# One broadcast of the packed slots per window, split into eight

## The chip, the cores and the metric

The kernel runs on one core of a Trainium2 chip. The metric is the device time of one execution in microseconds (us). Three executions of the kernel before took 478.18, 482.74 and 483.65 us; their median, 482.74 us, is what the change is compared with.

## The reference, cut to what matters

A graph layer over 6250 nodes with 128 features and 100000 edges that are sorted by destination (`dst`). Each edge has one of two types.

```python
Xs = X[src]
m_data = Xs @ W_data.T + b_data
m_ctrl = Xs @ W_control.T + b_control
msg = jnp.where((edge_types == 0)[:, None], m_data, m_ctrl)
agg = jax.ops.segment_sum(msg, dst, num_segments=X.shape[0])
out = agg + (X @ W_self.T + b_self)
x = _layernorm(X + jax.nn.relu(out), axis=-1)
```

## The kernel before, in words

**Messages first.** For all nodes and both types the products with the two weight matrices are computed once, in blocks of 128 nodes. The 98 blocks (49 for each type) stay in the tile `m3` as three bf16 parts of 128 columns each, which together carry the precision of float32, and are also written to a table in DRAM (L509). This is the first 60 us.

**Sums in two ways.** 27 windows of 160 destination nodes each are summed by matrices of zeros and ones (`ranks` and `sums`). The rest of the nodes are summed from rows that GpSimd gathers from the table by indirect transfers (`gathered`, L1027, 263 of them); their matmuls (L1034) lie between those of the windows.

**A window.** Windows are handled in eight groups: of one, of two, and six of four. For a group, `ranks` gives every edge a slot in a small list for each of the 98 source blocks, and leaves in the tile `vs` who stands in which slot. `put` (L772) writes `vs` to the DRAM tensor `packed`. For each window, `sums` then

- broadcasts that window's 32 x 98 slots to all 128 partitions of the tile `sp` (named "rows"): L904, a source of 6272 bytes written to each partition, 784 KB in all;
- lets VectorE compare `sp` with the partition's number, in two halves (L912), which gives 98 selection matrices of 128 x 32;
- lets TensorE multiply them with `m3` (stage 1, L933, 98 matmuls of 384 columns in 25 steps), ScalarE or VectorE copy each result to bf16 (L436, L437), and TensorE add these to the window's sums with a second selection, `hot2` (L920; stage 2, L947 and L950).

The tile `sp` has three buffers; a buffer is free when the stage-1 matmuls of the window three before are done. At the end `close` adds x, normalizes and stores.

**The order is planned.** All operations are entered with `add(engine, duration, function, due, reads, writes, lat)`. `Plan.run` walks through a modelled time: on each engine it takes, of the operations that are ready, the one with the smallest due time. Due times are priorities, not earliest starts. `lat` is the modelled delay until the result can be read. What comes out is a fixed order of instructions on each engine; the chip then waits on semaphores where the model was too quick. An operation on the SP queue (transfers) counts 0.45 us (`SPD`) in the model; a broadcast has `lat=2.0`. The due time of a window is `T0 + 13*w` with T0 = 36; its broadcast has due - 14 (`RA`), its compares due - 4 and due - 3.

Of the kernel before, what the change touches and what calls it, by code (L numbers as in the profile page):

```python
# [226 lines left out]
@with_exitstack  # L227
def kernel(ctx, tc, x, xt, edges, w, bias, out):
    nc = tc.nc
    const = ctx.enter_context(tc.tile_pool(name="const", bufs=1))  # L230
    total = const.tile([1, 1], I32, name="total")

    with ExitStack() as main:
        sums_over_windows(main, tc, x, xt, edges, w, bias, out, total)

    matched = nc.values_load(total[0:1, 0:1])
    with tc.If(matched != E), ExitStack() as rest:
        sums_over_all(rest, tc, x, xt, edges, w, bias, out)
# [9 lines left out]
def sums_over_windows(ctx, tc, x, xt, edges, w, bias, out, total):  # L248
# [23 lines left out]
    G0, G1 = 0.0, -4  # L272
    GC = 1.3
    SPD = 0.45
    RP, RA, RS = 1, 14, 0.9


    r0 = C([125, RH, 1], I32, "r0")
# [948 lines left out]
```

## Time and profile before

| What | us |
|---|---|
| median of three executions | 482.74 |
| the profiled execution, device time | 478.18 |
| its span, first to last instruction | 476.5 |
| TensorE busy with matmuls | 442.0 |
| VectorE busy | 393.0 |
| ScalarE busy | 354.1 |
| GpSimd busy | 298.4 |

The profiled execution is the fastest of the three; 1.7 us of its time lie outside its span. TensorE's granted clock is 0.99 of full speed in the mean. In the list of groups a line such as "L912 DVE TENSOR_SCALAR" names the line of the kernel, the engine and the operation; DVE is VectorE, ACT ScalarE, PE TensorE, POOL GpSimd. "SPq" is the queue that issues transfers in program order; a transfer that waits there holds back those behind it. In a timeline the columns are start, duration, engine, line, operation, tiles, form and count; a bracket at the end gives how long the engine stood idle before the instruction, and what ended it.

### The profile page before, as it was taken

How to read it: one execution, taken by the hardware profiler on the slowest of the kernel's cores; microseconds unless marked ns; L12 is line 12 of the kernel's file. 1: busy time of each engine (PE TensorE's matmuls, PEld its weight loads, DVE VectorE, ACT ScalarE, POOL GpSimd, SP SyncE). 2: the span in 40 equal slices, each digit the busy share in tenths (PEclk: the TensorE clock that was granted, in tenths of full speed). 3: DMA queues.
4: the chain of work that ended last, by engine and by line, in shares of the span. 5: the costliest groups of instructions: out<-in, count | busy, mean ns of one | idle time of the engine just before them, and what ended most of it. 6: DMA issues, size and time to landing. Idle time of an engine off the chain costs nothing.

```text
span 476.5 us, 26926 instructions
## 1 busy us (share of the span) xinstructions
PE 442.0 (93%) x11461; PEld 362.7 (76%) x11461; DVE 393.0 (82%) x1271; ACT 354.1 (74%) x891; POOL 298.4 (63%) x290
## 2 busy tenths in 40 slices
PE   4999988997999999999899999999999999999990
PEld 3666665775888878888788879888888887978970
DVE  6699979998999989989798998988969779554333
ACT  2476774766877976878777789777797778989981
POOL 1100017777777777777777776777777757777700
PEclk9999999999999999999999999999999999999996
DMA  5489977338463556644655446763466534746210
GB/s 147 122 233 356 300 238 211 106 91 272 142 194 83 173 180 181 186 114 112 196 183 172 113 119 186 201 179 101 124 178 191 165 84 118 229 145 182 80 44 20
DMA packets 63117, 76.83 MB, mean 161 GB/s; under 512 B 21000, under 2 KB 52893, under 8 KB 62989
## 3 DMA queue, kind: packets, MB, share of 16 engines
q1 hardware_dynamic: 49147, 47.35, 32.3%
q0 software_dynamic: 13456, 27.42, 21.7%
q8 instruction: 91, 1.49, 1.3%
q10 hardware_dynamic: 386, 0.26, 0.2%
q14 instruction: 37, 0.30, 0.2%
HBM read 60.50 MB, written 13.17 MB: 155 GB/s over the span
## 4 chain that ended last, share of the span: by engine, by line
PE 73%; DVE 10%; ACT 7%; DMA 6%; issue 2%; SPq 0%; ACTq 0%; DVEq 0%
PE g L933 20%; PE a L947 19%; PE rk L702 9%; PE ga L1034 7%; ACT gs L436 4%; PE a L950 3%; PE vt L752 3%; DMA t_msg<-table,t_idx 3%; PE g L493 3%; DMA rows<-packed 2%; DVE hot L920 2%; PE a L493 2%; ACT to_d L443 2%; DVE slot L716 2%; PE ga L702 1%
## 5 line engine op out<-in xcount | busy, mean ns | idle before, releaser
L1027 POOL DMA_INDIRECT t_msg<-table,t_idx x263 | 279.7, 1063 | 130.3 <-DVE hots L691 45.3
L436 ACT CAST gs<-g 128x384 bf16<-128x384 f32 x639 | 273.8, 481 | 73.2 <-PE g L933 55.7
L947 PE MATMUL a<-gs,hot 128*32 128x384 bf16 x2592 | 249.0, 328 | 7.7 <-ACT gs L436 5.1
L933 PE MATMUL g<-m,rows 128*32 128x384 bf16 x2646 | 253.0, 327 | 1.8 <-DVE rows L912 1.3
L933 PEld LDWEIGHTS <-rows 128*32 128x32 bf16 x2646 | 168.7, 134 | 13.1 <-DVE rows L912 1.6
L950 PE MATMUL a<-gs,hot 128*32 128x128 bf16 x1944 | 159.6, 219 | 0.2 <-issue 0.2
L947 PEld LDWEIGHTS <-hot 128*32 128x32 bf16 x2700 | 115.9, 95 | 33.9 <-issue 15.5
L1034 PE MATMUL ga<-t_msg,t_hot 128*32 128x384 bf16 x1036 | 102.0, 326 | 1.3 <-DMA t_msg<-table,t_idx 1.3
L716 DVE TENSOR_REDUCE slot<-rk 128x4 f32<-128x392 f32 (+1 forms) x138 | 76.3, 553 | 12.5 <-PE rk L702 9.8
L950 PEld LDWEIGHTS <-hot 128*32 128x32 bf16 x2025 | 82.5, 97 | 3.5 <-issue 0.4
L920 DVE TENSOR_TENSOR hot<-iota_b,to_d 128x1280 bf16<-128x1280 bf16 (+1 forms) x81 | 67.4, 842 | 0.0
L702 PE MATMUL rk<-hots,tri 128*32 128x392 bf16 (+1 forms) x588 | 59.9, 317 | 0.0
L702 PE MATMUL rk<-hots,rest 128*32 128x392 bf16 (+1 forms) x556 | 54.4, 320 | 4.9 <-DVE slot L716 3.2
L1034 PEld LDWEIGHTS <-t_hot 128*32 128x32 bf16 x1036 | 49.9, 97 | 5.5 <-issue 2.2
L912 DVE TENSOR_SCALAR rows<-rows,pid 128x1568 bf16<-128x1568 bf16 x54 | 34.2, 638 | 8.9 <-DMA rows<-packed 8.8
L691 DVE TENSOR_TENSOR hots<-iota_b,st 128x784 bf16<-128x784 bf16 (+1 forms) x83 | 38.9, 485 | 0.5 <-PE vt L752 0.4
L702 PEld LDWEIGHTS <-rest 128*32 128x32 bf16 x624 | 25.0, 96 | 14.2 <-issue 11.9
L561 DVE TENSOR_REDUCE s<-a 128x128 f32<-128x384 f32 x27 | 15.0, 556 | 24.5 <-ACT bs L436 11.0
L1021 DVE TENSOR_TENSOR t_hot<-iota_b,t_code 128x768 bf16<-128x768 bf16 (+2 forms) x47 | 24.6, 523 | 11.8 <-PE ga L1034 11.6
L702 PEld LDWEIGHTS <-tri 128*32 128x32 bf16 x672 | 28.5, 98 | 2.3 <-issue 0.2
L752 PEld LDWEIGHTS <-two 128*64 128x64 bf16 x567 | 14.4, 109 | 7.9 <-DVE two L743 3.2
L752 PE MATMUL vt<-hots,two 128*64 128x98 bf16 x546 | 17.1, 208 | 0.8 <-DVE two L743 0.4
(188 smaller groups left out, 527.1 us busy)
## 6 DMA issues: line engine op xcount, KB each, us to landing
rows<-packed SPq DMA_DIRECT2D x27, 784.0 KB
table<-m SPq DMA_DIRECT2D x12, 768.0 KB
t_msg<-table,t_idx POOLq DMA_INDIRECT x263
rows<-in_xt SPq DMA_DIRECT2D x8, 256.0 KB
xc<-in_xt SPq DMA_DIRECT2D x6, 320.0 KB
gl<-sr SPq DMA_DIRECT2D x27, 48.0 KB
xr<-in_x SPq DMA_DIRECT2D x5, 256.0 KB
out<-xr SPq DMA_DIRECT2D x5, 256.0 KB
```

The source lines that it names most:

```text
L436: [("ACT", act(cols), lambda: A.copy(o(), src())), ("DVE", dve(cols), lambda: V.tensor_copy(o(), src()))], None, None, due, r, w, lat)
L691: lambda k=k, kn=kn, ci=ci, hs4=hs4: V.tensor_tensor(hv(ci)[:, k - ks[ci] : k - ks[ci] + kn].rearrange("p k w (c d) -> p (k w) c d", d=2), ...
L702: T.matmul(acc.t[R * j : R * j + R, c * wide : c * wide + wide], wt.t[:, R * j : R * j + R], one(k).rearrange("p w c -> p (w c)"), start=s ...
L716: vec(due, len(m) * wide, lambda r=r, m=m: V.tensor_reduce(slot.t[:, r:KT:L, :], acc.t[:, : len(m) * wide].rearrange("p (k w c) -> p k w c ...
L752: T.matmul(vv()[q : q + 64, i // 2, :], two.t[:, (k - k0) * nw + i].rearrange("p f r -> p (f r)"), one(k)[:, i, :], start=k == 0 and i < 2 ...
L912: add("DVE", dve(half * NT, 0.335), lambda sp=sp, rs=rs: V.tensor_scalar(sp.t[:, rs], sp.t[:, rs], pid1.t, None, op0=ALU.is_equal), due - ...
L920: lambda i=i, hot2=hot2, s4=s4, c0=c0, c1=c1: V.tensor_tensor(hot2.t[:, c0:c1].rearrange("p g (c d) -> p g c d", d=2), iota1_b.t.rearrange ...
L933: T.matmul(gp.t[R * t : R * t + R, :D3], sp.t[:, :, 4 * g + t], m3.t[:, 4 * g + t, :], start=True, stop=True)
L947: T.matmul(a.t[R * j : R * j + R, :D3], hot2.t[:, g, R * j : R * j + R], gs.t, start=g == 0, stop=False, skip_group_check=True)
L950: T.matmul(a.t[R * c : R * c + R, D3:], hot2.t[:, g, P:], gs.t[:, c * D : (c + 1) * D], start=False, stop=last, skip_group_check=True)
L1027: add("POOL", GC, lambda m=m, kk=kk: G.indirect_dma_start(out=m.t, out_offset=None, in_=table[:, :], in_offset=bass.IndirectOffsetOnAxis(a ...
L1034: T.matmul(ga.t[R * i : R * i + R, :D3], hot.t[:, k % KB, R * i : R * i + R], m.t, start=k == 0, stop=False, skip_group_check=True)
```

## The change

One number differs: the broadcast of a window's slots is issued as eight transfers of 16 partitions each (98 KB) where it was one of 128 partitions. In the code `RP` goes from 1 to 8.

```diff
@@ -272,7 +272,7 @@
     G0, G1 = 0.0, -4
     GC = 1.3
     SPD = 0.45
-    RP, RA, RS = 1, 14, 0.9
+    RP, RA, RS = 8, 14, 0.9
```

`RP` is used in `sums` alone, at L903 to L908:

```python
for j in range(RP):
    add("SP", SPD, lambda i=i, sp=sp, j=j: S.dma_start(
        sp.t[P // RP * j : P // RP * (j + 1)].rearrange("p r c -> p (r c)"),
        packed[gi, i // 2, (i % 2) * 64 : (i % 2) * 64 + R, :]
        .rearrange("r c -> (r c)")[None, :].to_broadcast([P // RP, R * NT])),
        due - RA + RS * j, [(packed_b, gi)], [(sp, ("p", j))], lat=2.0)
```

Each piece is an operation of its own for the planner: 0.45 us of the SP queue, a due time of due - 14 + 0.9*j, and 2.0 us until it may be read. The compares of L912 read all of `sp`, so they come after the last piece. Since the order of every engine comes out of the planner, the order of other instructions can change too.

## The prediction

> **What bounds the kernel now.** I read the page's busy times first, then the engines by stretch, then the waits, then the SP queue's timeline around the broadcasts.
>
> ```profile
> span 476.5 us, 26926 instructions
> PE 442.0 (93%) x11461; PEld 362.7 (76%) x11461; DVE 393.0 (82%) x1271; ACT 354.1 (74%) x891; POOL 298.4 (63%) x290
> ```
> ```profile
> 0.00:60.00 60.00, 53.42 (x750) 34.35 (x752) 50.25 (x207) 33.42 (x70) 4.05 (x13) 1.00 0.76 232
> 60.00:125.00 65.00, 56.84 (x1487) 43.87 (x1483) 59.51 (x194) 43.55 (x116) 43.96 (x41) 1.00 0.63 184
> 125.00:440.00 315.00, 306.81 (x8581) 263.23 (x8576) 270.12 (x818) 253.74 (x648) 240.78 (x227) 1.00 0.55 156
> 440.00:477.00 37.00, 24.94 (x666) 21.23 (x655) 13.08 (x55) 23.34 (x61) 9.60 (x10) 0.87 0.18 49
> ```
> In the second view the columns after the length are busy PE, weight load, DVE, ACT, POOL, then clock, DMA share and GB/s. TensorE is the bound: from 125 to 440 us it idles 8.2 us in 315. Idle time worth having lies before 125 us (6.6 + 8.2) and in the tail (12.1), which the change does not touch. So a better broadcast can win little, and a worse one can cost as much as it pushes into TensorE.
>
> ```profile
> DVE rows L912 <- DMA rows<-packed: 8.8, 6, 2.7
> ```
> ```profile
> SPq L904 <- PE g L933: 48.9, 14, 12.1
> SPq L904 <- DMA packed<-vs: 14.1, 6, 3.3
> SPq L544 <- DMA rows<-packed: 2.2, 1, 2.2
> ```
> Most broadcasts wait in the queue for their buffer (48.9 us); the first of each group waits for `packed` (14.1 us), and there VectorE waits for the broadcast: 8.8 us in six places. How far that reaches TensorE differs:
>
> ```profile
> 70.96 0.63 DVE L912 TENSOR_SCALAR rows<-rows,pid 128x1568 bf16<-128x1568 bf16 x1 [2.16 <-DMA rows<-packed]
> ...
> 116.00 0.63 DVE L912 TENSOR_SCALAR rows<-rows,pid 128x1568 bf16<-128x1568 bf16 x1 [0.85 <-DMA rows<-packed]
> ```
> ```profile
> 72.11 0.35 PE L702 MATMUL rk<-hots,rest 128*32 128x392 bf16 x4 [1.61 <-DVE slot L716]
> ...
> 117.71 0.55 PE L933 MATMUL g<-m,rows 128*32 128x384 bf16 x8 [1.34 <-DVE rows L912]
> ```
> Twice VectorE's wait became TensorE's: 1.61 us through the rank chain that follows it, 1.34 us directly. At 228 us VectorE waited 0.67 us and TensorE not at all (6.00 of 6.00 us busy from 223 to 229). I counted off each window's 98 stage-1 matmuls and took the time from the end of its second compare to the first of them. Windows 1, 3, 7, 11, 15, 19 and 23, the first of their groups, have 2.2, 0.1, 7.5, 7.6, 6.5, 4.8 and 4.1 us; all others have 10 to 22 us.
>
> **The change, part by part.** *Instructions.* 27 broadcasts become 216, 189 more on a queue that now issues 238. Two broadcasts back to back start 0.43 us apart (109.56 and 109.99), so 189 x 0.43 = 81 us more issue time, at least. The queue has room; what counts is the train at the start of a group. Its eighth piece starts 7p after the first, p being the spacing.
>
> *The price of a piece.* No row of this trace shows a transfer to 16 partitions with 6 KB each. Nearest are trains of four short transfers to few partitions:
>
> ```profile
> 138.63 1.90 SPq L541 DMA_DIRECT2D xr<-in_x  x4
> ...
> 195.39 5.72 SPq L541 DMA_DIRECT2D xr<-in_x  x4
> ...
> 292.00 3.53 SPq L868 DMA_DIRECT2D gl<-sr  x4
> ```
> That is 0.47, 1.43 and 0.88 us for each. The queue uses eight semaphores in turn (their numbers stand in the trace's records), and a transfer waits until the last one on its semaphore has landed, which is why L544 above waited for a broadcast that it has nothing to do with; so slow pieces also slow their own issue. Bounds: p = 0.43 (issue alone) to 1.43. I take 0.88: of the three trains its transfers are the largest (48 KB against 16 KB), though part of it is a wait for the gather. From issue to landing of a short transfer 2.9 us (`packed` issued at 62.57, the broadcast that waited for it at 65.49). The last piece then lands 7p + 2.9 us after the first issue: 5.9, 9.1 or 12.9 us. Now it is 5.4 (65.49 to 70.96), 6.4 (109.56 to 116.00) and 4.9 (223.35 to 228.21).
>
> [...]
>
> *First windows of a group*, p = 0.88. Window 1: 9.1 - 5.4 = 3.7 us later, less 2.2 of slack: 1.5. Window 3: 9.1 - 6.4 - 0.1 = 2.6. Windows 7, 11, 15: up to 4.2 later, covered. Windows 19 and 23, some 3 later, covered by 4.8 and 4.1. Sum 4.1 us. At p = 0.43 it is 0 (window 1 is 0.5 later, window 3 earlier by 0.5); at 1.43 it is 5.3 + 6.4 for these two and, from the landing records of the others, 0.4 + 1.3 + 1.7 + 2.8 for windows 11, 15, 19 and 23: 18.
>
> *VectorE's order.* The planner now holds the train for 8 x 0.45 + 2 = 5.6 us instead of 2.45 and sets the compares later by 3.15 us. For a first window the chip is then late by 9.1 - 5.6 = 3.5 us, before by 5.5 - 2.45 = 3.0: about even. For a group's second window, issued just behind, the plan says 16 x 0.45 + 2 = 9.2 us after the first issue, the chip 15 x 0.88 + 2.9 = 16.1: 6.9 late; before 2.9 planned, and landed at 8.7 (the trace's landing records, 8.1 to 9.3 in five of the six groups of four): 5.8 late. That is 1.1 us more of VectorE standing still, in six groups 7 us, with evictions and rank reductions queued behind the compare. By the rows above perhaps half of such a wait reaches TensorE: 3 us. At p = 0.43 the plan's wait is longer than the real one and the term vanishes; at 1.43 it is (24.4 - 9.2 - 5.8) x 6 / 2 = 28.
>
> *The same pieces elsewhere.* Where a broadcast waits for its buffer, the train costs 3 to 6 us more of the queue, hidden by 10 to 22 us of slack. Behind it stand loads of x (due 20 us ahead), edges for later groups, and `gl`, needed in a window's last step: nothing, unless p is over 1. Window 0's broadcast lies among the table's writes but has 13 us until stage 1. GpSimd's gathers share the DMA engines; it waits for DMA 4.9 us in all and otherwise for TensorE to free its 14 buffers, so slower gathers cost nothing at first.
>
> *Sum.* 4 + 3 = 7 us on the profiled execution: 478.2 becomes 485. The median stands 4.6 us above that execution, so I put 482.7 + 7 = 490.
>
> **Rivals.** *Faster: pieces at issue speed.* With p = 0.43 the landing is as now, but VectorE's compares are planned 3.15 us later, past most of the 8.8 us of waits, and what rank work comes forward fills them. TensorE gets back at most its idle time around the broadcasts: 0.8 + 1.8 (60 to 72 us), 2.0 (110 to 123.6) and 1.2 (161 to 169), 5.8 us: 477. For it: back-to-back issues really are 0.43 us apart, and pieces leave gaps in which gathers get through. Against: the 16 engines share out 16 partitions instead of 128. It decides below p of about 0.5, where 7p + 2.9 is under 6.4.
>
> *Even.* The pieces cost about 0.6 each: 7 x 0.6 + 2.9 = 7.1, 0.7 us late at window 3, nothing elsewhere, 1 to 2 us won back on VectorE. 480 to 486. Also what a broadcast hidden by the planner's new order would look like.
>
> *Much slower.* p over 1.1: the first windows cost 3 + 4 + 1, the second (15 x 1.1 + 2.9 - 15.0) x 6 / 2 = 13, 500 and more.
>
> That the change does not do what it says is excluded but for one point: pieces could be strung out by other transfers with due times between theirs; the first windows would be later still.
>
> **How the numbers follow.** Within 1% is about what a measurement of this kernel can tell from no change. Slower by p near 0.9: 0.46, range 486 to 497. Much slower: 0.07. Even: 0.27. Faster: 0.20. The range for 8 in 10 runs from the faster case's 477 to 500, the sum at p = 1.1. Faster by over 1% (below 477.9): 0.20. Within 1%: 0.28. Slower by over 1%: 0.52.
>
> **What would show it.** Right: at group starts a train of eight L904 over 6 us or more; compares of windows 1 and 3 some 3 us later after the first issue; more VectorE time behind "DMA rows<-packed" than 8.8 us; TensorE idle before 125 us up by 4 us. Wrong: trains of 3.5 us with that wait near zero, or TensorE's idle time moving where no broadcast stands, which would be the planner's new order and not the pieces.

## The result and the profile after

| | before | after |
|---|---|---|
| median, us | 481.02 | 533.76 (533.43 to 534.08) |
| ratio | | 1.1098, 95% interval 1.1023 to 1.1172 |
| profiled span, us | 476.5 | 531.8 |

Eight pieces made the kernel 11% slower; 490 us was forecast, with a range up to 500. (A fourth execution of the kernel before took 479.31 us, so its median is 481.02 here.) Lines of the page of the kernel before, then of the changed kernel:

```profile
PE 73%; DVE 10%; ACT 7%; DMA 6%; issue 2%; SPq 0%; ACTq 0%; DVEq 0%
...
L702 PE MATMUL rk<-hots,rest 128*32 128x392 bf16 (+1 forms) x556 | 54.4, 320 | 4.9 <-DVE slot L716 3.2
...
L912 DVE TENSOR_SCALAR rows<-rows,pid 128x1568 bf16<-128x1568 bf16 x54 | 34.2, 638 | 8.9 <-DMA rows<-packed 8.8
```

```profile
span 531.8 us, 27272 instructions
...
PE 460.0 (86%) x11461; PEld 367.1 (69%) x11461; DVE 394.9 (74%) x1274; ACT 354.2 (67%) x888; POOL 301.8 (57%) x290
...
PE 53%; DMA 22%; SPq 8%; DVE 7%; issue 4%; ACT 4%; ACTq 0%; DVEq 0%; POOL 0%
...
L912 DVE TENSOR_SCALAR rows<-rows,pid 128x1568 bf16<-128x1568 bf16 x54 | 34.8, 655 | 61.4 <-DMA rows<-packed 40.9
L702 PE MATMUL rk<-hots,rest 128*32 128x392 bf16 (+1 forms) x556 | 55.5, 330 | 28.6 <-DVE slot L716 27.8
```

The work of VectorE, ScalarE and GpSimd is unchanged to about 1%. What grew is idle time: VectorE stood 61.4 us ahead of the compares, before 8.9. (The page names other releasers for a third of it; but `sp` is the only tile written by a transfer that an L912 reads, and by the landing records each of these compares started within 1 us of the landing of its own last piece.) TensorE's idle time before rank matmuls went from 4.9 to 28.6 us. On the chain that ended last, whose shares the lines with "PE 73%" and "PE 53%" give, transfers went from 6% to 22% of the span. The span grew by 55.3 us: TensorE was idle for 37.3 us more and, with the same matmuls, busy for 18.0 us more. By stretch, columns as before:

```profile
60.00:125.00 65.00, 52.78 (x1352) 39.94 (x1348) 56.54 (x185) 38.58 (x103) 41.61 (x39) 0.97 0.71 150
125.00:440.00 315.00, 280.37 (x7418) 232.70 (x7414) 244.05 (x729) 216.53 (x550) 208.88 (x194) 0.97 0.65 137
```

TensorE idles 34.6 us from 125 to 440, where it idled 8.2; the prediction looked for 4 of its 7 us before 125. One window in the middle of a group, window 13, shows how it comes about. The SP queue and VectorE in the kernel before, then the SP queue, VectorE and TensorE in the changed kernel, each from its timeline:

```profile
237.19 0.34 SPq L904 DMA_DIRECT2D rows<-packed  x1
```
```profile
244.24 0.62 DVE L912 TENSOR_SCALAR rows<-rows,pid 128x1568 bf16<-128x1568 bf16 x1
```
```profile
257.15 1.30 SPq L904 DMA_DIRECT2D rows<-packed  x1
258.55 1.10 SPq L868 DMA_DIRECT2D gl<-sr  x2
259.70 4.13 SPq L904 DMA_DIRECT2D rows<-packed  x7
```
```profile
268.56 0.69 DVE L912 TENSOR_SCALAR rows<-rows,pid 128x1568 bf16<-128x1568 bf16 x1 [2.35 <-DMA rows<-packed]
...
270.42 0.55 DVE L716 TENSOR_REDUCE slot<-rk 128x4 f32<-128x392 f32 x1
```
```profile
271.03 0.45 PE L702 MATMUL rk<-hots,rest 128*32 128x392 bf16 x4 [2.25 <-DVE slot L716]
```

Before, the broadcast landed at 243.5, 0.7 us ahead of the compare, and VectorE did not stand. In the changed kernel the first piece was issued at 257.15, the last at 262.6, and it landed at 268.5. VectorE stood 2.35 us, and the rank reduction behind the compare released TensorE 2.25 us late. Window 13's own matmuls began at 293.4, over 20 us after its compares: the window had all the slack that the prediction counted. VectorE's order had 0.7 us.

### The profile page after: what moved, and what is told of

The parts are those of the page before. It is cut to its first block, busy times and chain, and to the rows that moved or that the text cites. A ratio compares the mean times of both kernels' runs of the same rounds, so it can differ in the third digit from the quotient of the medians.

```text
span 531.8 us, 27272 instructions
## 1 busy us (share of the span) xinstructions
PE 460.0 (86%) x11461; PEld 367.1 (69%) x11461; DVE 394.9 (74%) x1274; ACT 354.2 (67%) x888; POOL 301.8 (57%) x290
## 4 chain that ended last, share of the span: by engine, by line
PE 53%; DMA 22%; SPq 8%; DVE 7%; issue 4%; ACT 4%; ACTq 0%; DVEq 0%; POOL 0%
PE g L933 16%; DMA rows<-packed 15%; PE a L947 14%; PE rk L702 6%; SPq L904 6%; PE ga L1034 5%; PE a L950 3%; PE vt L752 2%; DVE rows L912 2%; ACT gs L436 2%; DMA sr<-table,at 1%; DMA packed<-vs 1%; PE g L493 1%; DMA xc<-in_xt 1%; DMA xr<-in_x 1%
## 5 line engine op out<-in xcount | busy, mean ns | idle before, releaser
L947 PE MATMUL a<-gs,hot 128*32 128x384 bf16 x2592 | 255.6, 335 | 10.8 <-ACT gs L436 4.8
L933 PE MATMUL g<-m,rows 128*32 128x384 bf16 x2646 | 258.4, 336 | 3.9 <-issue 2.9
L933 PEld LDWEIGHTS <-rows 128*32 128x32 bf16 x2646 | 163.6, 135 | 20.4 <-issue 6.1
L950 PE MATMUL a<-gs,hot 128*32 128x128 bf16 x1944 | 162.1, 222 | 4.3 <-issue 4.3
L947 PEld LDWEIGHTS <-hot 128*32 128x32 bf16 x2700 | 118.1, 97 | 42.4 <-issue 24.9
L950 PEld LDWEIGHTS <-hot 128*32 128x32 bf16 x2025 | 82.7, 98 | 11.1 <-issue 5.9
L716 DVE TENSOR_REDUCE slot<-rk 128x4 f32<-128x392 f32 (+1 forms) x138 | 76.2, 553 | 17.5 <-PE rk L702 13.0
L912 DVE TENSOR_SCALAR rows<-rows,pid 128x1568 bf16<-128x1568 bf16 x54 | 34.8, 655 | 61.4 <-DMA rows<-packed 40.9
L702 PE MATMUL rk<-hots,rest 128*32 128x392 bf16 (+1 forms) x556 | 55.5, 330 | 28.6 <-DVE slot L716 27.8
L702 PE MATMUL rk<-hots,tri 128*32 128x392 bf16 (+1 forms) x588 | 61.3, 326 | 0.0
L1034 PEld LDWEIGHTS <-t_hot 128*32 128x32 bf16 x1036 | 48.1, 98 | 6.2 <-issue 1.9
L861 POOL DMA_INDIRECT sr<-table,at x14 | 16.4, 1169 | 10.5 <-DVE at L849 4.5
```

What stands on the lines that cost most here:

```text
L702: T.matmul(acc.t[R * j : R * j + R, c * wide : c * wide + wide], wt.t[:, R * j : R * j + R], one(k).rearrange("p w c -> p (w c)"), start=s ...
L716: vec(due, len(m) * wide, lambda r=r, m=m: V.tensor_reduce(slot.t[:, r:KT:L, :], acc.t[:, : len(m) * wide].rearrange("p (k w c) -> p k w c ...
L912: add("DVE", dve(half * NT, 0.335), lambda sp=sp, rs=rs: V.tensor_scalar(sp.t[:, rs], sp.t[:, rs], pid1.t, None, op0=ALU.is_equal), due - ...
L933: T.matmul(gp.t[R * t : R * t + R, :D3], sp.t[:, :, 4 * g + t], m3.t[:, 4 * g + t, :], start=True, stop=True)
L947: T.matmul(a.t[R * j : R * j + R, :D3], hot2.t[:, g, R * j : R * j + R], gs.t, start=g == 0, stop=False, skip_group_check=True)
L950: T.matmul(a.t[R * c : R * c + R, D3:], hot2.t[:, g, P:], gs.t[:, c * D : (c + 1) * D], start=False, stop=last, skip_group_check=True)
```

## The experiments

The indented paragraphs are the expectations, recorded before the run they belong to. They name five theories: A, a piece to 16 neighbouring partitions is slow; B, the number of transfers on the SP queue costs; C, the planner's new order costs; D, VectorE stands at compares that the plan put too early; E, the pieces cost in some other way too.

"Lands" is the time from the first piece's issue to the last piece's landing, from the trace's semaphore records; medians over the first windows of the six groups of four, the second windows (counted from the first window's first issue) and the rest. "Wait" is VectorE's idle time ahead of L912 on the page. The waits are read from the profiled executions (of h1 485.8, of h3 529.8, of k2 506.0 us), the times are medians.

| run | lands: first, second, rest | wait | median | ratio, interval |
|---|---|---|---|---|
| before | 5.7, 8.9, 5.8 | 8.9 | 481.02 | |
| h1, order alone | 5.6, 8.3, 5.5 | 0.8 | 481.23 | 0.997, 0.9926 to 1.0015 |
| k2, four pieces | 7.2, 11.2, 8.6 | 30.5 | 499.88 | 1.0328, 1.0261 to 1.0396 |
| k1, columns mixed | 8.2, 13.2, 10.6 | 35.6 | 502.20 | 1.0336, 1.0249 to 1.0423 |
| g1, columns | 8.2, 13.1, 10.8 | 27.2 | 503.81 | one execution, beside 479.35 |
| h3, strided | 8.5, 14.4, 11.2 | 59.5 | 525.39 | 1.0859, 1.0759 to 1.0960 |
| after | 9.4, 16.0, 11.5 | 61.4 | 533.76 | 1.1098, 1.1023 to 1.1172 |
| h2, pieces alone | 9.8, 16.5, 8.9 | 67.4 | 536.12 | 1.1113, 1.1007 to 1.1220 |

**Order and pieces apart.** The planner's view and the transfers can be set separately. First edit (e3, f1, h1): the planner sees eight operations, and the first issues the whole broadcast.

```diff
-                add("SP", SPD, lambda i=i, sp=sp, j=j: S.dma_start(
-                    sp.t[P // RP * j : P // RP * (j + 1)].rearrange("p r c -> p (r c)"),
+                add("SP", SPD, lambda i=i, sp=sp, j=j: j or S.dma_start(
+                    sp.t.rearrange("p r c -> p (r c)"),
...
-                    .rearrange("r c -> (r c)")[None, :].to_broadcast([P // RP, R * NT])),
+                    .rearrange("r c -> (r c)")[None, :].to_broadcast([P, R * NT])),
```

Second edit (e4, f2, h2): one operation that issues eight pieces.

```diff
-            for j in range(RP):
-                add("SP", SPD, lambda i=i, sp=sp, j=j: S.dma_start(
+            for _ in range(1):
+                add("SP", SPD, lambda i=i, sp=sp: [S.dma_start(
...
-                    due - RA + RS * j, [(packed_b, gi)], [(sp, ("p", j))], lat=2.0)
+                    for j in range(RP)], due - RA, [(packed_b, gi)], [(sp, ("p", 0))], lat=2.0)
```

> The planner still sees eight operations, so the order on all four engines is that of the changed kernel, but the first issues one transfer to all 128 partitions and the other seven issue nothing. Theory A and theory B: about the kernel before, 476 to 490. Theory C (the new order alone): 515 to 540.

> The planner sees one operation, so the order on all four engines is that of the kernel before, but it issues the eight pieces of 16 neighbouring partitions. Theory A and theory B: as slow as the changed kernel or slower, 520 to 550, since the compares are planned 3.15 us sooner. Theory C: 478 to 495.

On the chip of these two runs and of e1 and e2, and on the one of f1 and f2, the kernel before took 695 us instead of 481, and all variants stood within 2.1% of it. These six runs decide nothing between the theories: e1 699.40, e2 708.27, e3 696.71, e4 699.54, f1 699.55, f2 700.80 us. VectorE's wait shows in them too, 25.5 us in f2 against 0.0 in f1, but TensorE was busy for only 77% of the span there.

> The order of the changed kernel with one transfer to all 128 partitions, once more, since the chip of the first four runs took 695 us for the kernel before and hid every difference. Theory A (16 neighbouring partitions are slow): within 2% of the kernel before, 474 to 490 where that takes 481. Theory C (the planner's new order): 515 to 540.

> The order of the kernel before with the eight pieces of 16 neighbouring partitions, once more. Theory A: 520 to 550 where the kernel before takes 481, with over 55 us of VectorE waiting ahead of its compares. Theory C: 478 to 495.

Once more where the kernel before took 482.47 us:

> The column pieces took 504 us beside 479: about half of the loss goes with the 16 neighbouring partitions (A), half is left to eight transfers on the queue (B) or to the planner's new order (C). Here the order is the changed kernel's and there is one transfer to 128 partitions. C: 495 to 510, the half that the columns left. B: 474 to 488.

> The order of the kernel before, eight pieces of 16 neighbouring partitions. A and B together: 520 to 550, since pieces land some 9 to 11 us after the first issue where this order allows for 2.5. C: under 510, A's half alone.

Measured 481.23 and 536.12 us. In the traces VectorE, ScalarE and GpSimd run the same sequence of instructions in h1 as in the changed kernel, and in h2 as in the kernel before. The L912 group of h1 and of h2:

```profile
L912 DVE TENSOR_SCALAR rows<-rows,pid 128x1568 bf16<-128x1568 bf16 x54 | 34.5, 650 | 0.8 <-DMA rows<-packed 0.8
```
```profile
L912 DVE TENSOR_SCALAR rows<-rows,pid 128x1568 bf16<-128x1568 bf16 x54 | 35.0, 654 | 67.4 <-DMA rows<-packed 44.9
```

The new order costs nothing, and the pieces in the old order cost all of it. Theory C is out. h1 also ends the "faster" rival: the later compares took VectorE's wait from 8.9 to 0.8 us, and the time did not move.

**What makes the pieces slow.** Column pieces (e1, g1) send 4 of the 32 slot columns to all 128 partitions, with the same count, bytes and order. Strided pieces (e2, h3) go to every eighth partition.

```diff
-                    sp.t[P // RP * j : P // RP * (j + 1)].rearrange("p r c -> p (r c)"),
+                    sp.t[:, R // RP * j : R // RP * (j + 1)].rearrange("p r c -> p (r c)"),
```
```diff
-                    sp.t[P // RP * j : P // RP * (j + 1)].rearrange("p r c -> p (r c)"),
+                    sp.t[j::RP].rearrange("p r c -> p (r c)"),
```

(With the columns the source is cut in the same way: 4 slots, to 128 partitions.)

> Eight transfers per window as in the changed kernel, and the same planned order on TensorE, VectorE, ScalarE and GpSimd, but each writes 4 of the 32 slot columns (784 bytes) to all 128 partitions. If 16 neighbouring partitions are what makes a piece slow (theory A), a piece costs little more than its issue, the eighth lands about 6 us after the first issue instead of 9.2, VectorE's wait before the compares falls from 61 us to under 20, and the time is 478 to 492. If the number of transfers on the SP queue is the cost (theory B), or the planner's new order (theory C), it stays at 525 to 540.

> The changed kernel with each piece on every eighth partition (j, j+8, ...) instead of 16 neighbours: same order, same count, one run of 6272 bytes per partition as before. If neighbouring partitions share a way into the buffer (theory A, places), the spread halves or removes the sharing: 0.45 to 0.5 us for a piece, the eighth lands 6 to 7 us after the first issue, 480 to 505. If it is one long run per DMA engine that is slow, whatever the partitions (theory A, runs), or theory B or C, it stays at 520 to 540.

> The column pieces once more, one look, to see whether the chip is as quick as for the first measurement of both kernels. If the kernel before takes about 481 us beside it: theory A (16 neighbouring partitions are slow) 478 to 492; theory B (eight transfers on the queue) or C (the new order) 525 to 540. If the kernel before takes 695 again, it tells only the landing times of the pieces.

> The changed kernel with each piece on every eighth partition. If the neighbourhood of the 16 partitions makes a piece slow, about what the columns gave: 498 to 512. If a single run of 6272 bytes per DMA engine is slow wherever it goes, 525 to 540.

Measured 503.81 us for the columns and 525.39 for the strided pieces. The columns fell between their two ranges: with the same number of transfers 24 of the 53 us stayed (in one execution; k1 below agrees), so both A and the count or length of the train have a share. For h3 the neighbourhood's range missed by 13 us, and the time fell into the range for "a single run of 6272 bytes is slow wherever it goes". The packet records speak against that reading: a run of 6272 bytes took 0.24 us in the median before, 0.52 with 16 neighbours and 0.26 strided, so spreading does quicken the packets. But a strided piece takes longer to issue. L904 of the changed kernel and of h3, with durations in ns (least, median, most):

```profile
L904 SPq DMA_DIRECT2D rows<-packed x216: 302/418/1812, 29.1 to 488.5; - x108
```
```profile
L904 SPq DMA_DIRECT2D rows<-packed x216: 471/587/1767, 29.5 to 485.9; - x108
```

The train to the eighth issue was 5.1 us long instead of 3.9 in a group's first window. From the last issue to its landing 3.4 us passed instead of 5.5, and so the last piece landed at 8.5 instead of 9.4 us: about half of what came quicker, the issue took back.

The first compare needs only four of the column pieces, but all of the partition pieces. k1 sends the columns in the order 0, 4, 1, 5, 2, 6, 3, 7 to see whether that was their advantage; k2 sets RP to 4.

```diff
-            for j in range(RP):
+            for j, o in enumerate((0, 4, 1, 5, 2, 6, 3, 7)):
```
```diff
-    RP, RA, RS = 8, 14, 0.9
+    RP, RA, RS = 4, 14, 0.9
```

> The column pieces of e1 and g1 (504 us), the same plan, but issued in the order 0, 4, 1, 5, 2, 6, 3, 7, so the first compare needs the seventh piece. If the columns did better because a compare waited for four pieces only: VectorE waits 45 to 60 us ahead of L912 instead of 27, and 515 to 527, as with the strided pieces. If they did better because each reaches all partitions: 500 to 508.

> Four pieces of 32 neighbouring partitions (196 KB each). By the train (three spacings of about 0.46 us in place of seven, each piece twice as long) the last lands some 7.5 to 8.5 us after the first issue in a group's first window against 9.3 and 5.7; the planner allows 3.8. VectorE's wait 25 to 40 us, 495 to 515. If it is only the sixteen neighbours that hurt: under 488.

Measured 502.20 and 499.88 us. The mixed columns moved the wait from the second compare to the first and made it 35.6 us, less than the 45 to 60 expected, but cost no time: the four-piece explanation falls. Pieces to all partitions are better in themselves, 502.20 and 503.81 us in the two orders against 533.76. Four pieces stand between one and eight, as expected; their train (1.3 us in a group's first window) and their packets (0.43 us) do so too, and this run does not tell the two apart.

**Lateness against the plan.** If VectorE's standing is the cost, the planner can avoid it by knowing the landing time. i1 is the changed kernel, i2 the kernel before, j1 the columns, each told; j2 tells it for the changed kernel only from window 3 on.

```diff
-                    due - RA + RS * j, [(packed_b, gi)], [(sp, ("p", j))], lat=2.0)
+                    due - RA + RS * j, [(packed_b, gi)], [(sp, ("p", j))], lat=6.0)
```

In i2 and j1 it is `lat=5.0`, in j2 `lat=6.0 if w0 >= 3 else 2.0`.

> The changed kernel with eight pieces of 16 neighbouring partitions, but the planner is told that a piece can be read 6 us after its issue instead of 2, so VectorE's compares stand about 4 us later in its order. If the loss is VectorE standing at compares that the plan put too early (theory D, lateness against the plan), the wait ahead of L912 falls from 61 us to under 20 and the time to 482 to 495. If the pieces cost in another way too (theory E: the DMA engines or the SP queue are held up for others, or the windows start late for TensorE itself), it stays over 510.

> The kernel before with one transfer, the planner told 5 us instead of 2 until it may be read. The order of the changed kernel took 8 us off VectorE's wait without a gain, so by theory D nothing is left to win: 476 to 485, within 1% of the kernel before. If telling the truth helps by itself: under 474.

> Eight column pieces to all 128 partitions, the planner told 5 us instead of 2. If the 24 us that columns still cost are VectorE's compares standing before the landing (theory D): wait ahead of L912 under 8 us and 482 to 492. If eight issues per window on the SP queue cost by themselves (theory B): 498 to 510.

> The changed kernel with the planner told 6 us from window 3 on, 2 us for windows 0 to 2 as there. Theory D with a start of its own: window 3 about 6 us late as in the changed kernel, 10 us more after it, 493 to 503. If the start's loss was not due to the order of the first groups: 508 to 520.

| run | wait | median | ratio, interval | stage 1 of window 3 begins | last stage 1 less that |
|---|---|---|---|---|---|
| before | 8.9 | 481.02 | | 118 | 345 |
| after | 61.4 | 533.76 | 1.1098, 1.1023 to 1.1172 | 124 | 394 |
| i1, told | 9.2 | 514.92 | 1.0649, 1.0537 to 1.0762 | 134 | 362 |
| j2, told from window 3 | 10.3 | 510.44 | 1.0646, 1.0566 to 1.0727 | 130 | 362 |
| j1, columns told | 5.4 | 492.16 | 1.0236, 1.0175 to 1.0297 | 127 | 351 |
| i2, one transfer told | 3.4 | 483.77 | 1.0024, 0.9983 to 1.0065 | 120 | 348 |

The last two columns are in us of the profiled executions. The L912 group of i1:

```profile
L912 DVE TENSOR_SCALAR rows<-rows,pid 128x1568 bf16<-128x1568 bf16 x54 | 33.4, 635 | 9.2 <-DMA rows<-packed 8.9
```

i2 came as expected and j1 at the upper edge of theory D's range. i1 missed that range, 482 to 495, and lies in theory E's, over 510: D holds for a part of the loss. From window 3 on, the changed kernel lost 49 us against the kernel before, 32 with TensorE idle and 17 with TensorE busy longer. Told, it loses 17 (11 idle, 6 busy longer), the columns, told, 6, and one transfer, told, 3: there some 32 of 49 us went with the standing compares. Before window 3 the told pieces were behind the changed kernel by 3 to 10 us. In i1 a part of that has a place, the waits of TensorE from 60 to 140 us:

```profile
PEld L947 <- DMA gl<-sr: 6.7, 1, 6.7
PE a L947 <- DMA gl<-sr: 6.0, 1, 6.0
```

It is one stop of 6.0 us at the `gl` load of window 0; in the changed kernel it is 2.6 us. The load was issued behind 14 pieces, 2.2 us after its source had landed, and took 6.8 us to land, 3.6 in the changed kernel. TensorE's clock also stood at half speed for 15.0 us before window 3, 3.4 there. j2 was to spare the start; its stop was 2.7 us, but it still reached window 3 at 130 us, so the expectation of 493 to 503 missed and the other range, 508 to 520, came. Why telling the later windows delays the start stays open; so do the last 17 us.

## Why the prediction was wrong

- **Landing of a train: right in the sum, by luck.** 9.1 us was forecast for the last piece of a first window and 9.4 came. But the sum was seven issues 0.88 us apart and 2.9 us from the last issue to its landing; measured were issues 0.56 us apart (a train of 3.9 us, forecast 6.2) and 5.5 us to the landing. The two errors cancel. What stood 0.89 us apart were the landings (mean of a train, median of the six first windows): 100352 B in 0.89 us are 113 GB/s. No run here shows what sets that rate.
- **First windows: right in kind.** Stage 1 of window 3 began 6 us later, forecast 1.5 + 2.6; 2.1 us of it are the later landing of window 3 itself (8.5 us after the first issue, before 6.4). VectorE's wait in the six first windows was 7.5 us, before 5.4: "about even" held.
- **Second windows: mis-sized.** 7 us more of VectorE's wait were forecast, from a mean lateness against the plan; 15.7 us came, before 0. The landing was right (16.1 forecast, 16.0 measured), but lateness against the plan is not waiting: 5.8 us of it had cost no wait before.
- **"The same pieces elsewhere": the step that failed.** It put the twelve other windows of those groups at nothing, hidden by 10 to 22 us of slack. That slack is TensorE's, between compare and first matmul. The compare stands at a fixed place in VectorE's order, and there the slack was smaller: before, it started 0.03 to 4.0 us after the landing in ten of these windows, 7.6 and 7.7 us in two, and VectorE waited 1.4 us in all; after, 33.0. The last piece landed 11.5 us after the first issue instead of 5.8. Their trains were also longer than those of first windows, 6.0 us against 3.9; in window 13 other transfers stand in between, and in h2, where nothing does, the train was 3.3 us.
- **"Perhaps half of such a wait reaches TensorE": too low.** The wait grew by 52.5 us and TensorE's idle time by 37.3. From window 3 on, 21.1 us of that idle time are rank matmuls that waited for the reduction L716, which stands behind compares in VectorE's order. No fixed share follows: k1 waited 8 us longer than g1 in about the same time, and i1, with the old wait of 9 us, was still 6.5% slower. That 52.5 us of wait and 52.7 us of time agree is chance; 18.0 us of the time are TensorE's longer busy time, a term that the sum did not have.
- **Signs and rivals.** More wait behind the broadcast, and 4.1 us more of TensorE's idle time from 60 to 125 us, came as the sign said; the train of 6 us at group starts did not. "Much slower" had the size, but not by its condition: pieces landed 0.89 us apart, not over 1.1.
- **One sum was off.** At p = 1.1 the prediction's own terms give 21 us, 504 on the median's base, not 500. 534 lies outside either way.
- **The planner's new order**, named as what a wrong forecast might show, costs nothing (h1).
- **The faster rival** was right that later compares take away the waits, and that was worth nothing: 8.1 us less in h1 and 5.5 in i2 moved the time by 0 within the interval. Pieces at issue speed were not reached: they landed 0.89 us apart, where two issues back to back stood 0.43 us apart before.

## What to carry to other kernels

Slack has to be looked up on the engine that waits: a transfer that the consumer needs 20 us later still stops the engine between them, if its instruction stands there in a fixed order (window 13: 2.35 us of VectorE). Cutting one transfer into eight made the last byte arrive later, at 8.2 us with pieces to all partitions and at 9.4 with pieces to 16 neighbours, where one transfer took 5.7. In a planned schedule, change a transfer and its modelled landing time together, and try the order and the transfer apart.

## What the runs showed of the hardware

A piece to 16 neighbouring partitions took 0.42 us to issue in the median, one to every eighth partition 0.59. TensorE's granted clock was 0.99 in the mean before, with 34.5 us idle, and 0.967 after, with 71.8 us idle. In the changed kernel it stood at half speed in nine spells, eight of them 3.4 us long, instead of one, and TensorE's busy time went from 442.0 to 460.0 us for the same matmuls. On two other occasions the unchanged kernel took 695 us with a mean clock near 0.91. The traces there are of variants. f1 and h1 are the same kernel, 699.55 and 481.23 us: ScalarE's casts took 481 ns in both, but TensorE's weight loads for L947 waited 127.0 us in e3, the same kernel again at 696.71 us, for nothing that the profile shows, 13.7 in h1. No run here says why.
